# Source tiles of 8 by 16 and column halves for the weighted sums of a local-attention kernel

## The chip, the cores and the metric

The kernel runs on one core of one Trainium2 chip. The engines of that core work side by side: TensorE (PE; PEld is its weight load), VectorE (DVE), ScalarE (ACT), GpSimd (POOL) and SyncE (SP), each of which takes its instructions in the order in which they were written down for it, and DMA queues that are filled by SP and POOL. They meet at semaphores. The metric is the time of one execution on the device in microseconds, as the median of several runs; the profile is one further execution, recorded instruction by instruction.

## The reference

The input x has 4 images of 256 channels and 64 x 64 pixels, all in fp32. Two layers follow.

```python
# layer 0: attention weights from a dilated 7x7 convolution, then a weighted sum of shifted pixels
k = lax.conv_general_dilated(x, w1, window_strides=(1, 1), padding=[(6, 6), (6, 6)],
                             rhs_dilation=(2, 2), dimension_numbers=DN) + b1[None, :, None, None]
k = lax.conv_general_dilated(k, w2, window_strides=(1, 1), padding=[(0, 0), (0, 0)],
                             dimension_numbers=DN) + b2[None, :, None, None]      # 49 logits per pixel
attn = jax.nn.softmax(k, axis=1)
xp = jnp.pad(x, ((0, 0), (0, 0), (6, 6), (6, 6)))
shifts = jnp.stack([xp[:, :, 2*u:2*u + 64, 2*v:2*v + 64] for u in range(7) for v in range(7)], axis=1)
y = jnp.einsum('bkchw,bkhw->bchw', shifts, attn)
# layer 1: whitening in 4 groups of 64 channels (covariance over all pixels, five Newton steps)
```

Each output pixel of layer 0 is the sum of 49 source pixels, two rows or columns apart, weighted by the 49 softmax values of the output pixel. Layer 1 needs the mean and the 64 x 64 covariance of each group over all pixels of y and applies one 64 x 64 matrix per group.

## The kernel before

Because of the dilation of two, rows and columns of one parity only meet their own parity. An image falls into four quarters of 32 x 32 pixels; with 4 images there are 16 quarters, numbered n = 0 to 15. A slot in on-chip memory holds one row parity of one image, `[128, 2, 32, 64]` (channel, channel half, row, column with both column parities); five slots exist, and the results y are written over x in the same slot.

**Logits.** w1 and w2 are folded into one 7x7 kernel with 49 outputs, and the convolution is done by a two-dimensional transform: for each image, a list of row points (`row_eval`), for each of them seven column points (`col_ops`, written to the tiles `xh`), small matmuls on TensorE (`conv_bank`, L538; two groups of 49 output partitions, one per row parity, issued in turn), and the way back on VectorE (`interpolate`, with tiles `pv` and `zz`). One row point, the one at infinity, is done without the column transform by `direct` (L685): 14 terms (7 taps, 2 channel halves) of one matmul of up to 8 x 64 columns for each parity. Image 0 is done first, its row points 0, 4 and 5 also by `direct`; then images 1 to 3 in turn.

**Softmax.** `softmax(b, pc)` brings the logits of one column parity of an image to pixels on partitions (transposes on TensorE, L879), takes the maximum (VectorE), the exponentials (ACT, L893) and multiplies by the reciprocal sum and by `cmask`, which is zero where a column shift would leave the image. The result is a tile `d` with, per pixel, the 49 weights.

**Weighted sums.** For a quarter n, `move_terms` copies the weights of `d` to the tile `zt`, ordered by source row (10 copies, L941 and L953), and one SP DMA writes `zt` to a DRAM buffer `sd[n % 2]`. `load_band` reads it back with a row step one element shorter than it was written (L994, four DMAs for each of three parts), which shifts each source column against the last one, into the tile `band`; a VectorE transpose of 32 x 32 blocks (L1009, one per part) then puts source pixels on partitions and output pixels along the free axis. `make_block(n, m)` transposes 4 source rows of 32 columns of x on TensorE (L1032) and copies them to a tile `xb` (L1040; four buffers), so that source pixels are on partitions there, too. `weighted_sum` (L1061) multiplies the two into PSUM: for each half of 16 output rows five pieces, `PIECES`, each two matmuls, one per channel half. `store_y` (L1080, L1078) evicts the half into the slot, `turn_y` (L1093, L1101) transposes y to pixels on partitions and `moments` (L1114) adds up the covariance.

**The order of the work.** `first_half(n)` and `second_half(n)` write down the order around these parts: which block is made before which sum, and when the next quarter's terms and bands are loaded. They are set between the convolution steps of the next image by a plan with costs; the quarters of images 2 and 3 run partly and wholly after the last convolution, as do `finish` and the tail. TensorE's order is kept as written; on the other engines a scheduler sorts by priority. `load_x` (L130) loads a slot from POOL's queue, image 0 alone by SP's queue at the start. When images 0 and 1 are done, `move` writes slots 0, 1 and 2 out to DRAM (`spill`) and loads the remaining x into them; `bring_back` loads y again at the end. The last stage applies the whitening matrices (L1445, L1461), evicts on ACT and VectorE in turn and stores.

## Time and profile before

| | |
|---|---|
| runs of the kernel (us) | 745.49, 747.77, 745.45; median 745.49 |
| the profiled execution: span (us), taken as its time | 745.9 |
| TensorE busy, share | 704.8 us, 94% |
| VectorE busy, share | 609.9 us, 82% |
| ACT busy, share | 332.0 us, 45% |
| POOL busy, share | 50.8 us, 7% |
| y matmuls (L1061) on TensorE | 154.2 us in 640 records |
| block transposes of the bands (L1009) | 47.5 us, 48 |
| mean granted TensorE clock | 0.980 |

The page of a profile gives the busy time of each engine, then the span in 40 slices, the DMA queues, the chain of work that ended last (followed back from the last instruction, at each step to what released it), and groups of instructions with their mean duration and the idle time ahead of them. Matmuls are pipelined and their ends are modelled, so the busy time of TensorE overlaps; the distance between two starts tells more. Image 0's logits take until about 157 us, the softmax of image 0 and the first weighted sums follow; the last convolution ends at about 580 us, the last weighted sum at 673, the Newton steps at 690.

### The profile page before, as it was taken

The page shows a single profiled execution, that of the slowest core. Times are in us where ns is not written, and L with a number is a line of the kernel's source. Part 1 is how long each engine was busy: PE and PEld are TensorE (multiplying, and loading weights), DVE is VectorE, ACT ScalarE, POOL GpSimd, SP SyncE. Part 2 cuts the span into 40 slices and gives each one's busy share as a digit, 9 for nine tenths or more (in the row PEclk, how much of TensorE's full clock was granted, in tenths as well). Part 3 has the DMA queues.
Part 4 walks back from the last instruction along what each step waited for, and adds up shares of the span by engine and source line. Part 5 has one row for each costly group of instructions (what it writes and reads, how often), then busy time and mean ns, then how long its engine had stood idle before and what let it go on. Part 6 is the DMA issues. An engine that isn't in the chain of part 4 may idle for free.

```text
span 745.9 us, 18571 instructions
## 1 busy us (share of the span) xinstructions
PE 704.8 (94%) x7544; PEld 529.3 (71%) x7544; DVE 609.9 (82%) x1271; ACT 332.0 (45%) x955; POOL 50.8 (7%) x54
## 2 busy tenths in 40 slices
PE   6999999997998897999999999999999889998996
PEld 1449543376898794699998967899998678885331
DVE  3799997999999888877995999799969665545575
ACT  1424340255354443366445344736435563322564
POOL 0410070020000110001000100000000000000000
PEclk9999999999999998999999999999999999997899
DMA  8991110147262392056635920533422143372587
GB/s 322 258 307 73 71 78 19 65 134 227 71 224 91 121 317 62 20 194 211 223 113 172 295 70 2 164 110 111 165 74 86 46 149 107 111 268 103 217 362 323
DMA packets 59629, 114.41 MB, mean 153 GB/s; under 512 B 22887, under 2 KB 42008, under 8 KB 58776
## 3 DMA queue, kind: packets, MB, share of 16 engines
q1 hardware_dynamic: 55848, 94.36, 38.1%
q0 software_dynamic: 3696, 18.88, 7.3%
q8 instruction: 59, 0.97, 0.5%
q14 instruction: 26, 0.21, 0.1%
HBM read 65.88 MB, written 47.33 MB: 152 GB/s over the span
## 4 chain that ended last, share of the span: by engine, by line
PE 66%; DVE 26%; ACT 5%; issue 2%; DMA 1%; SPq 0%; DVEq 0%; ACTq 0%
PE cv L538 22%; PE y L1061 14%; PE acc L685 6%; PE tp L1445 4%; PE tp L1093 3%; PE sig L1114 3%; PE tp L1032 3%; PE cv L685 3%; DVE xh L313 3%; DVE pv L313 2%; DVE zz L313 2%; PE cv L222 2%; DVE ct L313 2%; DVE ct L306 2%; DVE band L1009 2%
## 5 line engine op out<-in xcount | busy, mean ns | idle before, releaser
L538 PE MATMUL cv<-xh,wr 128*49 128x128 f32 x4368 | 249.5, 275 | 5.7 <-DVE rm L899 5.3
L538 PEld LDWEIGHTS cv<-xh,wr 128*49 128x49 f32 x4368 | 243.4, 124 | 9.6 <-ACT xh L494 5.6
L1061 PE MATMUL y<-band,xb 128*128 128x224 f32 (+2 forms) x640 | 154.2, 380 | 8.5 <-ACT xb L1040 6.8
L1061 PEld LDWEIGHTS y<-band,xb 128*128 128x128 f32 x640 | 111.2, 196 | 31.0 <-ACT xb L1040 9.6
L548 ACT COPY pv<-cv 113x486 f32<-113x486 f32 (+1 forms) x63 | 30.0, 476 | 86.5 <-PE cv L538 86.4
L1080 ACT ACTIVATE slot<-y,pivot 128x512 f32<-128x512 f32 x53 | 36.7, 739 | 67.1 <-PE y L1061 67.0
L1101 ACT COPY yt<-tp 128x256 f32<-128x256 f32 x128 | 45.6, 378 | 38.4 <-PE tp L1093 37.0
L313 DVE SCALAR_TENSOR_TENSOR pv<-pv 113x162 f32<-113x162 f32 x186 | 55.4, 322 | 0.8 <-ACT pv L548 0.3
L1032 PE MATMUL tp<-ident,slot 128*128 128x128 f32 x256 | 49.8, 297 | 6.4 <-ACT yt L1101 6.4
L1009 DVE STREAM_TRANSPOSE band<-band 128x864 f32<-128x864 f32 (+1 forms) x48 | 47.5, 992 | 9.7 <-DMA band<-sd 7.3
L1093 PE MATMUL tp<-ident,slot 128*128 128x128 f32 x256 | 51.9, 299 | 3.7 <-ACT yt L1101 1.0
L1093 PEld LDWEIGHTS tp<-ident,slot 128*128 128x128 f32 x256 | 41.2, 205 | 13.8 <-issue 4.2
L1032 PEld LDWEIGHTS tp<-ident,slot 128*128 128x128 f32 x256 | 39.9, 205 | 12.7 <-ACT yt L1101 7.7
L941 ACT COPY zt<-d 32x112 f32<-32x112 f32 (+2 forms) x156 | 44.8, 287 | 1.9
L893 ACT ACTIVATE d<-tp,mx 128x49 f32<-128x49 f32 x128 | 37.0, 336 | 17.4 <-DVE mx L888 13.9
L313 DVE SCALAR_TENSOR_TENSOR xh<-ct 128x512 f32<-128x512 f32 x42 | 27.9, 686 | 13.8 <-PE cv L538 13.4
L1114 PEld LDWEIGHTS sig<-yt 128*64 128x64 f32 x1024 | 32.5, 138 | 6.3 <-issue 4.7
L1114 PE MATMUL sig<-yt 128*64 128x65 f32 x1024 | 36.9, 225 | 0.0
L1040 ACT COPY xb<-tp 128x256 f32<-128x256 f32 x87 | 30.5, 376 | 13.0 <-PE tp L1032 12.5
L1040 DVE COPY xb<-tp 128x256 f32<-128x256 f32 x41 | 16.5, 422 | 22.8 <-PE tp L1032 22.8
L685 PE MATMUL acc<-slot,tap 128*49 128x496 f32 (+3 forms) x168 | 34.6, 569 | 0.0
L893 ACT ACTIVATION_READ_ACCUMULATOR d<-tp,mx 128x1 f32 x128 | 30.7, 241 | 0.0
(228 smaller groups left out, 957.2 us busy)
## 6 DMA issues: line engine op xcount, KB each, us to landing
out_dram<-out SPq DMA_DIRECT2D x32, 512.0 KB, 3.5
sd<-zt SPq DMA_DIRECT2D x16, 896.0 KB, 4.2
slot<-in_x_dram POOLq DMA_DIRECT2D x12, 1024.0 KB, 10.8
band<-sd SPq DMA_DIRECT2D x128, 84.0 KB, 2.1
wr<-gd SPq DMA_DIRECT2D x15, 588.0 KB, 3.7
wr<-gd SPq DMA_DIRECT2D x15, 490.0 KB, 3.9
spill<-slot POOLq DMA_DIRECT2D x3, 2048.0 KB, 7.5
back<-spill SPq DMA_DIRECT2D x3, 2048.0 KB, 13.6
```

Source lines behind the costliest of these rows:

```text
L313: return in_turn(STT(o, a, f, b, ALU.mult, ALU.add))
L538: nc.tensor.matmul(cv[h * HB : h * HB + KT, k, sr : sr + n, sc : sc + n], wv[:, sc, sr, cc], xh[bc][:, :n, h * NCC + cc, :n], start=(j == ...
L685: nc.tensor.matmul(ps[h * HB : h * HB + KT, :, w0:w1_], w[v][:, cc], xs[:, :, cc, w0 + d : w1_ + d], start=(j == 0), stop=(j == len(order) ...
L893: nc.scalar.activation(d[:, h, i], lt[i // NI][:, i % NI, h, :KT], AF.Exp, bias=mx[:, i, h : h + 1], accum_out=s[:, h, i : i + 1],)
L941: ins = nc.scalar.copy(o, i)
L1009: return nc.vector.transpose(f, f)
L1032: nc.tensor.transpose(t[:, cc * P : (cc + 1) * P], xt[:, cc, CR * m : CR * (m + 1), bass.ds(pc, SW, 2)], ident,)
L1040: (nc.vector.tensor_copy if tail else nc.scalar.copy)(xb, t[:, :C])
L1061: nc.tensor.matmul(ps[:, cc, q0 - half * HALF : q1 - half * HALF, :], xb[:, cc * P : (cc + 1) * P], rhs, start=(k == 0), stop=(k == len(PI ...
L1093: nc.tensor.transpose(t[:, cc * P : (cc + 1) * P], yt[:, cc, CR * i : CR * (i + 1), bass.ds(pc, SW, 2)], ident,)
L1101: nc.scalar.copy(yb.rearrange("p a g c -> p (a g) c")[:, :, :GW], t[:, :C].rearrange("p (e c) -> p e c", c=GW),)
L1114: nc.tensor.matmul(sig[g * GW : (g + 1) * GW, cc], yb[:, cc, g, :GW], yb[:, cc, g], start=(count[0] == 0 and cc == 0), stop=(count[0] == 4 ...
```

## The change

The diff touches four things.

- **Tiles of the weighted sums.** Source blocks become 8 rows by 16 columns. A tile (t, h), t = 0 to 3 and h = 0, 1, contributes to 11 output rows and 19 output columns of one half (`ROW0`, `COLS`), so a half has four such pieces; a fifth one, "z", joins the three rows of source that lie over the border between the halves: its block is put together from the lower or upper 64 pixels of the two middle tiles by two further ACT copies.
- **Shift of the terms.** After the softmax, six VectorE shuffles move the weights of the seven column taps by -3 to 3 places within the 32 partitions, in place. `zt` has rows of 22, eight SP DMAs write it to a larger `sd` (cleared once at the start), and `load_band` reads tiles that already have source pixels on partitions: eight DMAs of `[128, 242]` and four of `[64, 3, 19]` per quarter. The block transposes are gone.
- **x in column halves.** A slot is laid out as channel half, column half, row, 32 columns. `load_x` issues four DMAs in place of two; image 0 is first loaded as before and used for its logits, and its two slots are loaded again in the new layout by POOL's queue after `row_eval(0, 5)`. `direct` splits each matmul of images 1 to 3 at the border of the column halves. The last stage reads and writes through views of the halves.
- **Smaller parts.** `row_eval` joins the two channel halves in one instruction for images 1 to 3; `xh` loses its padding column and its clearing on POOL; the eviction of `cv` leaves out the padding of the point at infinity, which makes two ACT copies of one.

```diff
+    TR8, TC = 8, SW // 2
+    WS = 22
+    TROWS = TR8 + R
+    ROW0 = (0, TR8 - R, 2 * TR8, 3 * TR8 - R)
+    COLS = ((0, TC + R), (TC - R, SW))
+    LS = 2 * KS * WS
+    RS = TC * (LS - 1) + WS
+    HS = SH * RS
...
-            queue.dma_start(store[s][:, cc], src[:, :, pr, :])
+            for h in range(2):
+                queue.dma_start(
+                    halves(store[s])[:, cc, h], src[:, :, pr, h * SW : (h + 1) * SW]
+                )
...
-            last = nc.scalar.copy(
-                pv[:K2, slot[b, br], i0 : i0 + len(pts)].rearrange("p n q b -> p (n q b)"),
-                cv[:K2, : len(pts)].rearrange("p n q b two -> p (n q b two)"),
-            )
+            full_ = len(pts) - (INF in pts)
+            nc.scalar.copy(
+                pv[:K2, slot[b, br], i0 : i0 + full_].rearrange("p n q b -> p (n q b)"),
+                cv[:K2, :full_].rearrange("p n q f -> p (n q f)"),
+            )
+            if INF in pts:
+                last = nc.scalar.copy(
...
             for h in range(2):
...
+                    xs = halves(slots[2 * b + h])[:, cc].rearrange("p h (q a) w -> p a h q w", a=4)
+                    parts = []
+                    for g in range(2):
+                        i0, i1 = max(w0 + d, g * SW), min(w1_ + d, (g + 1) * SW)
+                        parts.append(
+                            (i0 - d, i1 - d, xs[:, a, g, :, i0 - g * SW : i1 - g * SW])
+                        )
+                for k, (o0, o1, rhs) in enumerate(parts):
+                    pe(
+                        nc.tensor.matmul(
+                            ps[h * HB : h * HB + KT, :, o0:o1],
+                            w[v][:, cc],
+                            rhs,
...
     row_eval(0, 5, [rb[0], rb[1], xrs[5]])
+    for s in range(2):
+        load_x(s, s, nc.gpsimd)
...
+    for t in sd:
+        flat0 = zt.rearrange("p e w -> p (e w)")
...
+            nc.sync.dma_start(D0[:, f0:f1], flat0[:, : f1 - f0])
...
+        dv = d.rearrange("p h i (u v) -> p (h i u) v", u=KS)
+        for v in range(KS):
+            if v != R:
+                last = nc.vector.stream_shuffle(
+                    dv[:, :, v], dv[:, :, v], [(c - v + R) % SW for c in range(SW)]
+                )
...
-        nc.sync.dma_start(
-            sd[n % 2].rearrange("(p f) -> p f", p=P),
-            zt[:, R : R + NCH * KS].rearrange("p e w -> p (e w)"),
-        )
+        D = sd[n % 2][:]
+        for g in range(CR):
+            for h in range(2):
+                p0 = g * SW + h * TC
+                nc.sync.dma_start(
...
+        for t in (2 * half, 2 * half + 1):
+            e = ROW0[t] - TR8 * t + R
+            for h in range(2):
+                dma = nc.sync.dma_start(
+                    band[:, t, h].rearrange("p r w -> p (r w)"),
+                    bass.AP(
+                        tensor=D.tensor,
+                        offset=D.offset + h * HS + TR8 * t * RS + e * WS + COLS[h][0] - h * TC + R,
+                        ap=[[LS - 1, P], [1, TROWS * WS]],
+                    ),
+                )
...
-        def turn_blocks():
...
-                return nc.vector.transpose(f, f)
...
         xb = bpool.tile([P, C], F32, tag="xb", name=f"xb_{n}_{t8}{h}", bufs=4)
         with tc.high_priority():
             (nc.vector.tensor_copy if tail else nc.scalar.copy)(xb, t[:, :C])
         blocks[n, m] = xb
+        if t8 in (1, 2):
+            z = ("z", 2 - t8)
+            if h == 0:
+                blocks[n, z] = bpool.tile([P, C], F32, tag=f"xbz{t8}", name=f"xbz_{n}_{t8}")
+            i = slice(0, 64) if t8 == 2 else slice(64, P)
+            with tc.high_priority():
+                nc.scalar.copy(blocks[n, z][h * 64 : (h + 1) * 64], t[i, :C])
...
     PIECES = (
-        ((1, 1, 11), (0, 0, 7), (2, 5, 15), (3, 9, 16), (4, 13, 16)),
-        ((4, 16, 23), (3, 16, 19), (5, 17, 27), (6, 21, 31), (7, 25, 32)),
+        ((0, 0), (0, 1), (1, 0), (1, 1), ("z", 0)),
+        (("z", 1), (2, 0), (2, 1), (3, 0), (3, 1)),
     )
...
+        if m[0] == "z":
+            q0, nq = (HALF - R, R) if half == 0 else (0, R)
+            c0, c1 = 0, SW
+            rhs = bandz[:, half].rearrange("p r w -> p (r w)")
+        else:
+            q0, nq = ROW0[m[0]] - HALF * half, TROWS
+            c0, c1 = COLS[m[1]]
+            rhs = band[:, m[0], m[1], :, : c1 - c0]
...
-                    ps[:, cc, q0 - half * HALF : q1 - half * HALF, :],
+                    ps[:, cc, q0 : q0 + nq, c0:c1],
```

## The prediction

> **What bounds the kernel now.** I read the page's busy table first, then the chain of work that ended last, then one busy table over seven stretches, and last the timeline of single stretches, because a modelled "busy" does not tell how fast TensorE issues.
>
> ```profile
> PE 704.8 (94%) x7544; PEld 529.3 (71%) x7544; DVE 609.9 (82%) x1271; ACT 332.0 (45%) x955; POOL 50.8 (7%) x54
> PE 66%; DVE 26%; ACT 5%; issue 2%; DMA 1%; SPq 0%; DVEq 0%; ACTq 0%
> L1009 DVE STREAM_TRANSPOSE band<-band 128x864 f32<-128x864 f32 (+1 forms) x48 | 47.5, 992 | 9.7 <-DMA band<-sd 7.3
> ```
>
> ```profile
> 157.00:188.00 31.00, 25.28 (x430) 24.47 (x427) 31.00 (x62) 17.49 (x86) 5.32 (x7) 0.98 0.65 199
> 188.00:300.00 112.00, 103.39 (x1230) 88.66 (x1228) 105.19 (x232) 51.79 (x132) 7.29 (x9) 0.95 0.43 142
> 300.00:552.00 252.00, 249.13 (x3286) 220.02 (x3283) 219.01 (x433) 126.52 (x409) 7.87 (x6) 1.00 0.44 140
> 552.00:612.00 60.00, 54.54 (x576) 46.56 (x572) 48.41 (x114) 34.39 (x133) 1.14 (x7) 1.00 0.27 82
> 612.00:676.00 64.00, 62.39 (x549) 52.20 (x549) 30.70 (x61) 21.67 (x55) 0.00 (x0) 1.00 0.53 187
> ```
>
> The columns after the length are PE, PEld, DVE, ACT, POOL, granted clock, DMA share, GB/s. From 300 to 552 us and from 612 to 676 us TensorE hardly pauses; from 157 to 188 us VectorE is busy all the time; from 188 to 300 us the two take turns. So a microsecond of TensorE is worth most of a microsecond, a microsecond of VectorE only counts before 300 us. In the timeline, starts tell the issue rate (columns: start, us):
>
> ```profile
> 612.51 1.24 PE L1061 MATMUL y<-band,xb 128*128 128x320 f32 x4
> 613.59 0.39 PE L1093 MATMUL tp<-ident,slot 128*128 128x128 f32 x2
> ...
> 614.06 0.92 PE L1061 MATMUL y<-band,xb 128*128 128x224 f32 x4
> 614.82 0.39 PE L1093 MATMUL tp<-ident,slot 128*128 128x128 f32 x2
> ...
> 616.58 1.37 PE L1061 MATMUL y<-band,xb 128*128 128x224 f32 x8
> 617.88 1.15 PE L1114 MATMUL sig<-yt 128*64 128x65 f32 x32
> ```
>
> Each fp32 matmul leaves two records. Four records of 320 columns take 1.08 us (270 ns each), four of 224 take 0.76 (190 each): 0.845 ns per column either way. The last eight are four of 224 and four of 96: 1.30 - 0.76 = 0.54, so 96 columns cost 135 ns, a floor above 0.845 x 96 = 81. Two more places matter:
>
> ```profile
> 414.38 3.37 POOL L130 DMA_DIRECT2D slot<-in_x_dram  x2 [7.61 <-PE cv L538]
> ```
>
> ```profile
> 429.19 1.05 ACT L448 COPY rb<-slot 128x1024 f32<-128x1024 f32 x1 [1.70 <-DMA slot<-in_x_dram]
> ```
>
> ```profile
> 294.07 11.52 PE cv L685 x56
> ```
>
> ACT, which works in order, already waits 1.70 us for an x load; and one direct convolution of 28 matmuls takes 11.5 us.
>
> **The change part by part.** The profiled execution spans 745.9 us; I take that as its time, 0.4 us above the median of the three runs (745.49). The sum is made against 745.9.
>
> 1. Weighted sums. Before, each of the 32 halves has ten matmuls, two for each piece of 10, 7, 10, 7 and 3 rows of 32 columns: 20 records, 4 x (270 + 190 + 270 + 190 + 135) = 4.22 us. After, eight matmuls of 11 x 19 = 209 columns and two of 3 x 32 = 96: 209 x 0.845 = 177 ns, above the floor; 4 x (4 x 177 + 135) = 3.37 us. Saving 0.85 x 32 = 27.2 us of TensorE. Bounds: the 135 ns floor gives 4 x 5 x 135 = 2.70 us (a gain of 49); the other side is a penalty for runs of 19 columns. The nearest windows in the trace, the 8 x 58 ones of L685, start in pairs 0.387 us apart for 464 columns, 0.83 ns per column, no penalty. I take 27.2.
>
> [...] If a window cost what its 11 full rows of 32 cost (298 ns, an estimate), a half would take 5.31 us and the total would rise by 35 instead of falling by 27.
>
> 2. Direct convolutions of images 1 to 3 (the images are counted from 0) (L685, three times). Each matmul becomes two of one column half, issued first half, second half for one partition group of the output, then both for the other. Before, the two groups alternate and run together: 28 matmuls of 496 columns on average in 11.5 us equal 28 x 2 x 0.845 x 496 / 2. In the new order the second half of a group meets the first of the next, so pairs still run together but wait for the wider part: 2 pairs per term, 2 x 2 x 256 x 0.845 = 0.87 us, 14 terms 12.1, and one unpaired start 0.4: 12.6, so +1.1 x 3 = +3.3 us. No row shows two matmuls of one group in succession beside another group. Bounds: -0.5 us each, and nothing overlapping, 4 x 14 x 248 x 2 x 0.845 = 23.5 us, +36 in all. I take +3.3, as both orders in the trace (L538, L685) overlap completely.
>
> 3. Copies for the middle piece. 64 ACT copies of 64x256, by the row of 128x256 (376 ns) 24 us on ACT, which is 45% busy. TensorE waits only where the last piece of a first half follows its copy: the transpose's result is copied to xb, then to the z block, some 0.2 + 0.27 + 0.38 us, while one pair of 209-column matmuls covers 0.71. About 0.2 us for 12 n (in the last four VectorE copies xb beside ACT), 2.4, and I take 3 for ACT's other work in between; bounds 0 and, if both copies start only when that cover ends, 16 x 0.65 = 10. The cv eviction with the point INF splits in two (569 ns becomes about 430 + 280, x21): the second cv bank hides it.
>
> 4. VectorE. 48 block transposes go (47.5 us). 48 shuffles of 128x112 come, between the 128x56 row of L899 (0.21 us) and the 113x162 row of L313 (0.32): 0.24 each, 12 us. Merging row operations saves 30 pairs x 0.15 = 4. Before 188 us there are 12 shuffles and no transpose: +2.5 us on the path (0 to 3.8). From 188 to 300 us twelve transposes go (11.9 us); TensorE pauses there for some 9 us by the table, not all on VectorE, which limits the gain: -5. After 300 us TensorE covers it. Net -2.5, bounds +4 and -12.
>
> 5. x loads with rows of 128 B, POOL's queue. A 1 MB issue (1.7 us on POOL) becomes two of 4096 pieces each, so four issues per slot: 6.8 us of POOL instead of 3.4. Landing took 10.8 us (page 6). If time goes by bytes nothing is added but 3.4 us of issue, most under the transfer; if by pieces, it doubles, +10.8. The slot-2 load issued at 414.4 ended the ACT wait at 429.2, so all of it lands there; the one issued at 266 is used by ACT at 283.4, some 4 us after it landed. What queues behind that ACT copy: xh, pv evictions, yt copies; TensorE has a bank or so of work, about 4 us. I take +8 us of landing, being nearer to pieces: +4 at image 3, +2 at image 2; bounds 0 and 16. The 4 MB reload of slots 0 and 1 starts after row_eval(0, 5) (about 107 us), with 13.6 us of POOL issues, and is wanted at 194 us: even at 2 x 4 x 10.8 = 86 us it lands in time. The four DMAs that clear sd sit on SP before the weight loads of 162 us: 2.5 MB at the fastest rate in the page's slices (362 GB/s) is 7 us, starting near 157: at most 2 us late where VectorE has the path; nothing.
>
> [...]
>
> 6. SP's queue. Per n 13 issues become 20 (8 for sd, 12 band and bandz loads), 0.43 us each. In the last four n, after a second half: 6 loads 2.6, 8 writes 3.4, landing 2.1 (the 84 KB row), 6 loads 2.6, landing 2.1 = 12.8 us, against 15.7 us per n before and 14.0 after part 1. It fits. With the 4.2 us landing of the old sd write twice it is 17.0, +3 x 4 = 12. At the starts of images, where the softmax waits for shuffles (1.4 us) before zt is moved, I take +1.5.
>
> Sum: -27.2 + 3.3 + 3 - 2.5 + 6 + 1.5 = -16, so 730 us.
>
> **Rivals.** (a) The column halves of the direct convolutions do not overlap: -16 - 3.3 + 36 = +17, 763 us. Place: L685 at 143, 294 and 439 us. For: all three lie in TensorE-bound stretches (11.5 us on the chain at 294). Against: groups overlap fully today. It turns the sign when one costs 5.3 us more than the 1.1 assumed. (b) One of the DMA waits comes at its high end: x loads +10 or SP +12, so 740 to 742. For: the 1.70 us wait at 429 has no slack. Against: POOL is busy 7% of the span, and SP's sum of 12.8 us leaves 1.2 us of slack. (c) Both at once, or a new static order of ACT and SP in which weight loads queue behind band loads: 752. (d) 19-column windows run at the price of full rows: 730 + 62 = 792. Against: the 58-column windows. (e) VectorE's relief counts fully (-12) and POOL's loads go by bytes: 715. (f) The change doesn't bring what it says, for the freed TensorE time turns into waits for VectorE: around 745; against, VectorE is 87% busy from 300 to 552 us and loses 19 transposes (18.8 us) there for 24 shuffles (5.8).
>
> **How the numbers follow.** A measurement of this kernel tells 0.3% (2.2 us) from no change. Forecast 0.52 (own range 719 to 738); (b) 0.11; (e) 0.06; (f) 0.05; (c) 0.12; (a) 0.09; (d) 0.05. Faster: 0.52 + 0.11 + 0.06 = 0.69, less 0.05 because a change that rewrites the order on every engine can hide a cost that no row shows, 0.64; within 0.3%: 0.05; slower 0.31. To leave out no more than 2 in 10 the range goes from 713 to 764, with (a) and (c) inside and (d) outside.
>
> **What would show it.** y records of 128x209 start 177 ns apart; the direct convolutions take 12.6 us each on the chain; half periods in the tail fall from 7.85 to about 7.0 us; the ACT copy rb<-slot of image 3 waits about 9 us for DMA; VectorE is busy some 570 us; shuffles show about 0.24 us. Wrong it would be if direct convolutions show 17 us or more, if y records show over 200 ns, or if TensorE pauses appear ahead of the y matmuls with band or bandz as releaser.

## The result, and the profile after

The changed kernel takes 768.9 us (median; 762.4 to 772.0), the kernel before 745.8 (745.5 to 747.8) beside it: a ratio of 1.028, 95% interval 1.023 to 1.033. It is slower by 23 us, where 730 us and a range of 713 to 764 had been forecast. The profiled execution spans 768.6 us against 745.9. Of the kernels below, e_noshuf, f_shufh and b_shuf also had slow executions (two of four, two of ten and one of four), which the times and ratios given for them leave out.

The page's busy table and, under it, seven columns per stretch as in the prediction (PE, PEld, DVE, ACT, POOL, granted clock, DMA share, GB/s) show a TensorE with less work and more idle time:

```profile
PE 689.3 (90%) x7712; PEld 546.8 (71%) x7712; DVE 593.9 (77%) x1288; ACT 358.1 (47%) x1041; POOL 77.5 (10%) x68
```

```profile
157.00:188.00 31.00, 30.53 (x473) 28.16 (x470) 30.83 (x67) 13.64 (x55) 5.83 (x8) 1.00 0.80 244
188.00:300.00 112.00, 87.19 (x1154) 82.55 (x1151) 94.61 (x216) 55.12 (x169) 8.08 (x10) 0.88 0.48 136
300.00:552.00 252.00, 235.08 (x3162) 216.23 (x3158) 215.97 (x442) 134.09 (x434) 16.30 (x11) 0.97 0.49 133
...
612.00:676.00 64.00, 54.21 (x483) 48.23 (x482) 31.75 (x94) 36.54 (x138) 0.00 (x0) 0.92 0.42 90
```

From 188 to 300 us TensorE was busy 103 of 112 us before and is busy 87 now; from 300 to 552 us it is idle for 17 us where it was for 3, from 612 to 676 us for 10 where it was for 2. The granted clock is lower in the same stretches.

The part that the change is about did what was forecast. In the timeline of the changed kernel (start, duration in us), four records of 209 columns start 0.71 us before the next instruction, 177 ns each:

```profile
671.81 0.87 PE L1148 MATMUL y<-band,xb 128*128 128x209 f32 x4
672.52 0.39 PE L1108 MATMUL tp<-ident,slot 128*128 128x128 f32 x2
```

Where nothing else intervenes (the last three quarters), a quarter takes 13.97 us from first y matmul to first y matmul, against 15.72 before: 1.75 us saved, 28 us over sixteen quarters. I then went from half to half through both traces, and split each stretch into time with a TensorE instruction under way and time without. Over the whole span the time without grew by 38.0 us and the time with fell by 15.3, which makes the 22.6 us of the spans. So if the 27 us were saved, as the last quarters say, then 38 us of new pauses came, and some 12 us of the remaining work ran slower.

The table of what TensorE waited for (us in total, times, longest) names the pauses:

```profile
PE tp L1179 <- ACT yt L1187: 15.4, 8, 3.9
PE cv L574 <- DVE xh L326: 13.9, 2, 7.7
PE cv L574 <- DMA wr<-gd: 10.6, 1, 10.6
PE sig L1200 <- ACT yt L1187: 5.8, 2, 5.1
PE y L1148 <- ACT xb L1114: 5.7, 2, 5.5
PE y L1148 <- ACT xbz L1122: 4.4, 14, 1.4
```

Before, the longest was 5.3 us, and all of TensorE's waits together were 34 us against 71 now. Five places explain most of it.

**Image 0's loads (pause of 6.2 us at 51.6 us).** VectorE, which had its data at once before, waits twice for SP's loads of x, as its timelines show, first of the kernel before, then of the changed one (in brackets the idle time before and what ended it):

```profile
36.73 4.62 DVE L306 TENSOR_TENSOR rb<-slot 128x1024 f32<-128x1024 f32 x4
```

```profile
42.14 2.36 DVE L326 TENSOR_TENSOR rb<-slot 128x1024 f32<-128x1024 f32 x2 [5.33 <-DMA slot<-in_x_dram]
50.54 2.36 DVE L326 TENSOR_TENSOR rb<-slot 128x1024 f32<-128x1024 f32 x2 [6.04 <-DMA slot<-in_x_dram]
```

These loads were not touched. But POOL, which before spent 4.12 us on clearing seven `xh` tiles, now starts its loads of slots 2 and 3 at 29.5 us instead of 33.4, and they move through the same 16 DMA engines (over the span the packets of SP's queue take 41.1% of their time, those of POOL's 11.2%), whose mean busy share from 0 to 60 us is 0.96. POOL's timeline:

```profile
29.52 5.17 POOL L143 DMA_DIRECT2D slot<-in_x_dram  x3
```

**Weights behind bands (10.6 us at 189.8 us).** In the timeline of SP's queue (start, duration) eight `sd` writes and twelve band loads stand ahead of the weights for the next convolution bank. The kernel before comes first, the changed one second:

```profile
169.35 0.32 SPq L954 DMA_DIRECT2D sd<-zt  x1
...
174.34 8.76 SPq L994 DMA_DIRECT2D band<-sd  x12
183.20 11.20 SPq L378 DMA_DIRECT2D wr<-gd  x4
```

```profile
182.50 6.00 SPq L1034 DMA_DIRECT2D sd<-zt  x8
189.48 0.82 SPq L1067 DMA_DIRECT2D band<-sd  x2
...
194.82 1.23 SPq L1078 DMA_DIRECT2D bandz<-sd  x2
196.16 12.30 SPq L398 DMA_DIRECT2D wr<-gd  x4
```

The weights stood behind twelve band loads before, too, and from the first `sd` write to the weights the queue takes as long as it did (13.7 us against 13.9). What is new is that this stretch begins 13 us later: image 0's logits reach TensorE for the softmax 8.3 us later (163.77 us against 155.47), and six shuffles, from 177.07 to 180.52 us, stand between the softmax and `zt`. TensorE itself is only some 8 us late, so it waits 10.6 us; before, it waited 5.3 there, for VectorE.

**Shuffles ahead of ACT's copies (at 349, 495, 624 and 638 us).** At 636 us VectorE starts a softmax's six shuffles, and ACT, which has the `zt` copies of their result next in its fixed order, stands still, with the `yt` copy behind them; that is what TensorE waits for. The timelines of VectorE, ACT and TensorE of the changed kernel in turn:

```profile
635.88 0.57 DVE L971 TENSOR_TENSOR d<-d,rm 128x392 f32<-128x392 f32 x1
636.49 0.01 DVE L977 LOAD_MASK_SELECT d<-d  x1
636.49 0.64 DVE L977 STREAM_SHUFFLE d<-d 128x112 f32<-128x112 f32 x1
...
638.94 0.92 DVE L977 STREAM_SHUFFLE d<-d 128x112 f32<-128x112 f32 x1
```

```profile
639.93 1.78 ACT L1017 COPY zt<-d 32x112 f32<-32x112 f32 x6 [3.67 <-DMA bandz<-sd]
641.62 0.37 ACT L1187 COPY yt<-tp 128x256 f32<-128x256 f32 x1
```

```profile
642.03 0.70 PE L1179 MATMUL tp<-ident,slot 128*128 128x128 f32 x2 [3.89 <-ACT yt L1187]
```

ACT's wait is put down to a DMA, but that had long landed; it ends as the last shuffle does (638.94 + 0.92). The shuffles start 0.55 us apart, not 0.24.

**VectorE behind (5.5 us at 211 us).** Here no `zt` copy is in the way. ACT has a copy to `xh`, which waits for VectorE's `rb`, ahead of the `xb` copy that TensorE needs, and VectorE works without a pause from 196 to 218 us, with six shuffles from 198.85 us on. The timelines of ACT and TensorE:

```profile
208.60 0.65 ACT L1114 COPY xb<-tp 128x256 f32<-128x256 f32 x2
215.92 0.66 ACT L516 COPY xh<-rb 128x512 f32<-128x512 f32 x1 [6.67 <-DVE rb L333]
```

```profile
216.91 1.76 PE L1148 MATMUL y<-band,xb 128*128 128x209 f32 x4 [5.49 <-ACT xb L1114]
```

**A turn-taking of VectorE and TensorE (7.7 us at 254 us).** VectorE's order has changed so that it is idle while TensorE runs the last quarter's sums, and prepares the next bank when TensorE has nothing else. It is there in every version of the changed kernel below, with 2.6 us in e_ztpool and 7.7 to 9.6 us in the others. The half with it is 8.0 us longer than before, the next one 5.5 us shorter, so its net price is some 2.5 us.

A long pause cost more than itself here. After the pauses of 10.6, 5.5 and 7.7 us TensorE's granted clock is 0.50 for 4 to 5 us, as the figure after POOL's busy time shows for the changed kernel around the pause of 211.4 to 216.9 us:

```profile
211.00:217.00 6.00, 0.51 (x5) 0.32 (x3) 5.86 (x6) 1.05 (x3) 0.00 (x0) 0.86 0.02 8
217.00:221.00 4.00, 4.00 (x14) 3.75 (x15) 4.00 (x5) 2.36 (x7) 0.00 (x0) 0.50 0.00 0
221.00:225.00 4.00, 4.00 (x60) 3.67 (x61) 4.00 (x4) 3.61 (x11) 0.00 (x0) 0.86 0.00 0
225.00:229.00 4.00, 4.00 (x70) 3.82 (x64) 4.00 (x7) 3.27 (x11) 0.00 (x0) 1.00 0.41 73
```

From 217 to 221 us 14 matmul records are there, from 225 to 229 us 70. The half with this pause is 7.4 us longer than before, of which 5.5 are the pause and 1.9 slower work.

After a pause of 2.8 us, at 349 us, the granted clock was 0.50 as well:

```profile
352.00:355.00 3.00, 3.00 (x10) 2.61 (x9) 2.35 (x8) 2.26 (x7) 0.00 (x0) 0.50 0.40 69
```

### The profile page after: what moved, and what is told of

Read it like the earlier page. It is cut to its first block, busy times and chain, and to the rows that moved or that the text cites. A ratio compares the mean times of both kernels' runs of the same rounds, so it can differ in the third digit from the quotient of the medians.

```text
span 768.6 us, 19234 instructions
## 1 busy us (share of the span) xinstructions
PE 689.3 (90%) x7712; PEld 546.8 (71%) x7712; DVE 593.9 (77%) x1288; ACT 358.1 (47%) x1041; POOL 77.5 (10%) x68
## 3 DMA queue, kind: packets, MB, share of 16 engines
q1 hardware_dynamic: 84840, 94.42, 41.1%
q0 software_dynamic: 5040, 23.07, 11.2%
## 5 line engine op out<-in xcount | busy, mean ns | idle before, releaser
L574 PE MATMUL cv<-xh,wr 128*49 128x128 f32 x4368 | 249.9, 277 | 25.0 <-DVE xh L326 13.9
L1148 PE MATMUL y<-band,xb 128*128 128x209 f32 x512 | 117.5, 358 | 5.8 <-ACT xb L1114 5.7
L1148 PEld LDWEIGHTS y<-band,xb 128*128 128x128 f32 x512 | 91.6, 203 | 7.3 <-ACT xb L1114 6.4
L1179 PE MATMUL tp<-ident,slot 128*128 128x128 f32 x256 | 53.6, 307 | 19.2 <-ACT yt L1187 15.4
L585 ACT COPY pv<-cv 113x486 f32<-113x486 f32 (+2 forms) x63 | 27.4, 436 | 90.2 <-PE cv L574 80.1
L143 POOL DMA_DIRECT2D slot<-in_x_dram x32 | 54.0, 1692 | 79.9 <-issue 30.8
L1179 PEld LDWEIGHTS tp<-ident,slot 128*128 128x128 f32 x256 | 41.1, 205 | 28.8 <-ACT yt L1187 17.7
L1108 PE MATMUL tp<-ident,slot 128*128 128x128 f32 x256 | 50.8, 304 | 0.0
L958 ACT ACTIVATE d<-tp,mx 128x49 f32<-128x49 f32 x128 | 37.3, 335 | 18.0 <-DVE mx L953 15.5
L1200 PEld LDWEIGHTS sig<-yt 128*64 128x64 f32 x1024 | 33.3, 139 | 12.3 <-ACT yt L1187 6.1
L739 PE MATMUL acc<-slot,tap 128*49 128x256 f32 (+7 forms) x224 | 34.8, 468 | 0.0
L455 ACT ACTIVATE wr<-wr 128x392 f32<-128x392 f32 (+1 forms) x36 | 17.3, 513 | 33.7 <-DVE wr L326 24.0
L326 DVE TENSOR_TENSOR ct<-rb 128x1024 f32<-128x1024 f32 (+1 forms) x24 | 26.6, 1114 | 7.5 <-ACT rb L481 7.1
```

What stands on the lines that cost most here:

```text
L143: queue.dma_start(halves(store[s])[:, cc, h], src[:, :, pr, h * SW : (h + 1) * SW])
L574: nc.tensor.matmul(o, wv[:, sc, sr, cc], xv[bc][:, h * NCC + cc], start=(j == 0), stop=(j == len(terms) - 1), skip_group_check=True,)
L739: nc.tensor.matmul(ps[h * HB : h * HB + KT, :, o0:o1], w[v][:, cc], rhs, start=(j == 0 and k == 0), stop=(j == len(order) - 1), skip_group ...
L958: nc.scalar.activation(d[:, h, i], lt[i // NI][:, i % NI, h, :KT], AF.Exp, bias=mx[:, i, h : h + 1], accum_out=s[:, h, i : i + 1],)
L1108: nc.tensor.transpose(t[:, cc * P : (cc + 1) * P], tile_of(xt, cc, t8, h, pc), ident)
L1148: nc.tensor.matmul(ps[:, cc, q0 : q0 + nq, c0:c1], xb[:, cc * P : (cc + 1) * P], rhs, start=(k == 0), stop=(k == len(PIECES[half]) - 1), s ...
```

## The experiments

All times are medians, beside runs of the kernel before on the same chip (745.8 to 747.7). "The changed kernel" is at 768.9 us; its own runs differ by 10 us and the interval of its ratio spans 7 us, so a gain against it is known to some 5 us.

### e_memset: POOL's loads start later again

```diff
         xh[b] = apool.tile([P, Q8 * 2 * NCC * Q8 * 2], F32, name=f"xh{b}")
+        nc.gpsimd.memset(xh[b], 0.0)
```

> The changed kernel with the seven xh memsets put back on POOL ahead of its x loads of slots 2 and 3; the order on every other engine stays as it is. Theory A (the loads of slots 2 and 3 start some 4 us earlier once these memsets are gone, and share the DMA engines with SP's loads of image 0): the loads start near 33 us instead of 29.5, SP's loads of image 0 end near 38 to 40 us instead of 49.96, the two DVE waits of 5.33 and 6.04 us for slot<-in_x_dram nearly go, the first y matmul comes 6 to 8 us earlier, and the total falls by as much, to about 762 us. Rival (image 0's loads are late for another reason, or the time is lost again behind them): loads end near 50 us still, total within 2 us of 768.9.

Measured: 758.4 us, ratio to before 1.017 (1.012 to 1.022): 10.5 us less by the medians, by this one edit, which adds work to POOL and changes no other engine's order. In its profile POOL's loads start at 32.7 us, and VectorE's first wait is gone; the second remains:

```profile
36.74 2.36 DVE L327 TENSOR_TENSOR rb<-slot 128x1024 f32<-128x1024 f32 x2
45.59 2.36 DVE L327 TENSOR_TENSOR rb<-slot 128x1024 f32<-128x1024 f32 x2 [6.49 <-DMA slot<-in_x_dram]
```

Theory A holds in the main, though image 0's last load still lands near 45 us, not 38 to 40. TensorE's pause falls from 6.2 to 1.2 us and the first y matmul comes 4.9 us earlier; the two profiled spans differ by 6.0 us, so 6 of the 10.5 us are seen in a trace. In the other kernels that keep the early loads, the same pause took 2.9, 5.8, 7.1 and 10.3 us (e_ztpool, e_vmajor, e_noshuf, e_wrpool); in others with this edit VectorE's second wait took 0, 0.5, 3.1 and 4.2 us (e_three, f_vmajor, f_pool, f_shufh). Whether it depends on how the two streams of packets meet, and makes up a part of the changed kernel's spread of 10 us between runs, was not shown.

### b_half: column halves of x in the kernel before

```diff
-            queue.dma_start(store[s][:, cc], src[:, :, pr, :])
+            for h in range(2):
+                c = slice(h * SW, (h + 1) * SW)
+                queue.dma_start(store[s][:, cc, :, c], src[:, :, pr, c])
```

> The kernel before with one thing of the change: each x load of POOL is issued as two column halves, so in pieces of 128 B instead of 256 B, into the old layout; no other engine's order changes. Theory by pieces: the POOL packets of 4096 B take 278 ns as in the changed kernel instead of 194, a slot lands some 5 to 10 us later, the ACT copy rb<-slot of image 3 waits 6 to 10 us instead of 1.70, and the total rises by 4 to 8 us to 750 to 754. Theory by bytes, or hidden: the wait grows by no more than 3.4 us (the issue time of two more DMAs) and the total stays within 2 us of 745.8.

Measured: 749.9 us, ratio 1.0038 (1.0019 to 1.0056), so 2.9 us more. The ACT copy of image 3 waits 3.82 us instead of 1.70:

```profile
431.38 1.05 ACT L450 COPY rb<-slot 128x1024 f32<-128x1024 f32 x1 [3.82 <-DMA slot<-in_x_dram]
```

It lies between the two theories. The wait grew by 2.1 us, within the 3.4 us of issue time; the total moved by more than "hidden" allows. Pieces of half the size did not cost twice the time: POOL's packets of 4096 B took 274 ns on average in the changed kernel, which loads the same pieces, and 203 before, a third more. In the changed kernel the same copy waits 4.79 us.

### e_noshuf: no shuffles

```diff
-        for v in range(KS):
+        for v in range(0):
             if v != R:
                 last = nc.vector.stream_shuffle(
```

> The changed kernel without the 48 partition shuffles (so the terms of each column are not shifted, and the weighted sums use wrong weights); the rest is computed as before. Theory B (each softmax's six shuffles take 3.1 us on VectorE, not 1.4, the zt copies in ACT's fixed order wait for them, and behind those the yt copies that TensorE needs): the TensorE pauses for yt at 349, 495, 624 and 638 us (2.8, 3.3, 1.8, 3.9 us) go, the total falls by 8 to 14 us, to 755 to 761. Rival (the shuffles are covered by TensorE's work, as the prediction had it; the pauses move to another releaser): the total falls by at most 3 us.

Measured: 737.2 us (733.4 and 741.1), ratio 0.987 (0.979 to 0.995); over all four runs the median is 743.3, the figure that later expectations start from. Leaving the shuffles out gives 31.7 us by the one and 25.6 by the other, at least twice what Theory B expected; VectorE's busy time falls by 25.1. By place, in the profiled execution (747.9 us), from half to half against the changed kernel: 7.6 us at the second half of the sums (the pause at 211 us), 7.0 at 493 to 545 us, 9.0 at 612 to 649. The edit also changes the order on VectorE, ACT and SP, so a part of this can be the order. The pause at 349 us is the one that merely moved: 2.8 us stand at 353 us, with the next convolution bank as the waiting step.

### e_wrpool: image 1's weights on POOL's queue

```diff
-            nc.sync.dma_start(wt, gd[br][:, s0 : s0 + ns])
+            (nc.gpsimd if b == 1 else nc.sync).dma_start(wt, gd[br][:, s0 : s0 + ns])
```

> The changed kernel with the weight loads of image 1 (wr<-gd) issued by POOL instead of SP. Theory C (the weights wait in SP's queue behind eight sd writes and the band loads of image 0): the 10.6 us pause of TensorE at 189.8 us falls to about 5, the wait that the kernel before has there on VectorE; total falls by 4 to 6 us, to about 764. Rival (the transfer itself is late, or VectorE would have held TensorE as long): the pause stays at 9 to 11 us under another releaser, total within 2 us of 768.9.

Measured: 757.6 us, ratio 1.012 (1.006 to 1.019): 11.3 us less, above the 4 to 6 of Theory C. The pause at 189.8 us is halved, as expected, which is 5.7 us, and the one of 5.5 us at 211 us is gone as well. The edit also changes the fixed orders of VectorE and ACT, so what the second part is due to stays open. The line of TensorE's timeline with the first pause:

```profile
198.95 7.64 PE L574 MATMUL cv<-xh,wr 128*49 128x128 f32 x96 [4.96 <-issue]
```

### e_ztpool and f_pool: the zt copies on POOL

```diff
-                    ins = nc.scalar.copy(o, i)
-                    if after is not None:
+                    ins = nc.gpsimd.tensor_copy(o, i)
+                    if False:
```

The second line takes away an order that some of these copies had been given on ACT. f_pool has this together with the edits of e_memset and e_wrpool.

> The changed kernel with all of ACT's zt copies (terms to the staging tile) made by POOL; the shuffles stay on VectorE. It tells apart how the 25.6 us come that leaving the shuffles out gave. Theory B1 (ACT's fixed order: yt and xb copies stand behind zt copies that wait for the shuffles): TensorE's pauses for yt at 349, 495, 624 and 638 us (2.8, 3.3, 1.8, 3.9 us) go, total falls by 8 to 14 us to 755 to 761. Rival B2 (the shuffles' own 3.1 us of VectorE per softmax, 25 us for eight, count directly): the pauses stay with VectorE as releaser, total within 3 us of 768.9.

> The changed kernel with the xh memsets back, image 1's weight loads on POOL's queue, and the zt copies on POOL; everything is computed. Theory A + C + B1: 768.9 - 10.5 - 11.3 - 10 = 737, faster than the kernel before (747). Rival (POOL's copies are slower than ACT's, or stand behind its weight and x loads, so that bands come late): y matmuls wait for band<-sd, total 748 or more.

Measured: 774.3 us for e_ztpool, ratio 1.039 (1.033 to 1.045), and 765.8 for f_pool, 1.027 (1.023 to 1.030). The remedy failed for a reason that the rival of f_pool had named in part: POOL's copies took 723 ns on average against ACT's 289, so `zt` was ready later. But it was not the y matmuls that waited for their bands; the weights stood behind them in SP's queue. In e_ztpool the chain reads from POOL to SP:

```profile
177.35 17.59 POOL L1017 COPY zt<-d 128x56 f32<-128x56 f32 x11 [14.32 <-DVE d L977]
```

```profile
190.86 6.98 SPq L1034 DMA_DIRECT2D sd<-zt  x8
...
208.35 1.49 SPq L398 DMA_DIRECT2D wr<-gd  x3
```

TensorE paused 27.0 us there, for `wr`. The pauses for `yt` at 349, 495, 624 and 638 us did go, but 9.0 and 4.2 us at 356 and 508 us came in their place, ahead of convolutions that wait for weights, and 2.9 us at 639 us for `xbz`. So it does not decide between B1 and B2; it confirms C once more, with the other sign.

### e_three: the three causes taken away together

The edits of e_memset, e_wrpool and e_noshuf in one kernel.

> Three edits in one: the xh memsets back on POOL, image 1's weight loads on POOL's queue, and the shuffles left out (so the weighted sums use unshifted terms). If the three causes are separate, their gains add: 10.5 + 11.3 + 25.6 = 47.4, total 721 to 723. If they overlap (the 5.5 us pause at 211 us went both without shuffles and with the weights on POOL, 7.6 us of y offset each), total 728 to 732. Rival (TensorE's granted clock, 0.951 against 0.980, is a cost of its own): total not under 738, clock still at 0.95.

Measured: 725.5 us, ratio 0.973 (0.970 to 0.976), and a clock of 0.974. Singly the edits gave 47.4 to 53.5 us, by the two figures for e_noshuf, together 43.4: largely separate causes with an overlap of 4 to 10 us (the pause at 211 us, 7.6 us, counts in two of them). The rival falls: the clock came back with the pauses' end. Without the three, the change is worth 21 us, more than the forecast of 16, and this with shuffles left out.

### f_shufh, f_defer, f_noz: when the shuffles are made, and the copies for the middle piece

f_shufh (with the edits of e_memset and e_wrpool) makes the shuffles per half of a softmax:

```diff
-        dv = d.rearrange("p h i (u v) -> p (h i u) v", u=KS)
+            dv = d[:, h].rearrange("p i (u v) -> p (i u) v", u=KS)
```

f_defer also moves those of the second half into `second_half`:

```diff
+        if n % 4 < 2:
+            shuffle(n // 4, n % 4, 1)
         turn_y(n, 0)
```

f_noz is f_defer with the z copies taken out:

```diff
-        xb = blocks[n, m]
+        xb = blocks[n, {("z", 0): (1, 1), ("z", 1): (2, 0)}.get(m, m)]
...
-        if t8 in (1, 2):
+        if t8 in ():
```

> The changed kernel with the xh memsets back, image 1's weight loads on POOL's queue, and each softmax's shuffles made in two groups of six of 128x56, the first right after its half is normalized; everything is computed. If what counts is how soon the first half's terms can be copied to zt: 768.9 - 21.8 = 747 less up to 6 us, 741 to 747. Rival (a shuffle's price is mostly fixed, so twelve of them take 4.5 to 6 us per softmax instead of 3.1): 750 to 760.

> The changed kernel with the xh memsets back, image 1's weight loads on POOL's queue, and the shuffles in groups of six of 128x56 for half a softmax: those of the first half right after it is normalized, those of the second half only in the second half of the n two before they are wanted, when TensorE has other work. Everything is computed. If the shuffles cost by what waits for them at an image's start (some 20 of the 25.6 us, as the first half alone still costs f_shufh 744.2 against 725.5 without shuffles), putting half of them under cover gives half of these 18.7 us back: 733 to 738. Rival (their place does not matter, VectorE's own 0.3 us each times 96 does): 742 to 746, as f_shufh.

> As f_defer, but without the copies that gather the two middle pieces (the z pieces multiply the block of a neighbouring tile instead, so four rows and more of each half get wrong sums): the price of the 64 copies. By TensorE's waits for xbz (4.4 us for y, 2.3 for tp in the changed kernel) 5 to 8 us below f_defer; by the prediction's term, 3 us below; if the waits only move to the next releaser, within 1.5 us of it.

Measured: f_shufh 743.8 us, ratio 0.9964 (0.9940 to 0.9988); f_defer 742.4, 0.9942 (0.9922 to 0.9962); f_noz 736.5, 0.9854 (0.9825 to 0.9884). With two queues put right the changed kernel, all computed, is a little below the kernel before. Putting half of the shuffles elsewhere gave 1.4 us, which the two intervals do not tell from nothing, and not the 6 to 11 expected; VectorE's busy time is 595.5 and 595.3 us, the same. But the edit moved them far in image 0 only (to 207 and 225 us, from 171 and 194); in images 1 to 3 the second group begins 1.4 to 7.6 us after the first has ended, against 1.4 to 6.2 in f_shufh. So whether their place matters stays open. The copies for the middle piece cost 5.8 us, about what the waits for `xbz` show, where the prediction had 3.

### b_shuf2, b_shufout, b_copy, b_strout: what six instructions per softmax cost the kernel before

b_shuf and b_shuf2 are the same kernel; each partition is mapped to itself, so only time is added, in the chain from softmax to bands:

```diff
+        dv = d.rearrange("p h i (u v) -> p (h i u) v", u=KS)
+        for v in range(KS):
+            if v != R:
+                last = nc.vector.stream_shuffle(dv[:, :, v], dv[:, :, v], list(range(SW)))
```

b_copy has `tensor_copy` in place of the shuffle; b_shufout shuffles a contiguous tile of zeros, and b_strout one with steps of seven elements, both read by nobody else.

> The kernel before with six shuffles per softmax added after the normalization, in place and with each partition mapped to itself (the result is unchanged); the 48 block transposes stay. Theory B (in the chain softmax, zt, sd, band, y the shuffles' 3.1 us per softmax is paid at the images' starts): the total rises by 10 to 25 us over 746. Rival (it is the new static order that makes them cost, not the place): at most 4 us.

> The kernel before with six in-place shuffles per softmax that map each partition to itself, once more, for a look at where the 36 us are. By the first time: 780 to 786 us. Theory P (place: the chain softmax, zt, sd, band, y): TensorE's added pauses stand at the first y of each image and at the copies behind zt. Theory V (VectorE's time): the added pauses are ahead of cv matmuls whose inputs VectorE makes, before 300 us above all.

> The kernel before with six in-place copies of the same 128x112 shapes in the place of the shuffles (some 0.2 us each, 1.2 us per softmax, against 3.1). If the price goes by the time that they add, in the chain or on VectorE: about a third of 36 us, 755 to 762. If more instructions there mean a worse fixed order whatever they take: 772 to 784. If only the shuffle itself is dear: within 3 us of 747.

> The kernel before with the same number of shuffles of 128x112 per softmax on a tile of zeros that nothing else reads, so that no later step waits for them but VectorE's own order. Theory P: at most 5 us over 747. Theory V: the same 25 to 36 us as in the chain, 772 to 783.

> The kernel before with six shuffles per softmax on a tile of zeros that nothing else reads, now on 112 elements seven apart (28 B, over 112 neighbouring elements), so that they take as long as those of the change, off the chain of the bands. If time on VectorE is what they cost: 0.4 to 0.55 us each, 20 to 26 us of VectorE, total +20 to +37 (766 to 783). If the chain is what makes them cost: at most 10 us over 746. If the stride does not set their price: VectorE's busy time rises by 8 us as in b_shufout, total 752 to 755.

| kernel | time (us) | ratio to before | more than before (us) | VectorE's busy time added (us) |
|---|---|---|---|---|
| b_shuf | 783.6 | 1.047 (1.045 to 1.049) | 35.9 | |
| b_shuf2, shuffles in the chain | 783.1 | 1.049 (1.045 to 1.052) | 37.3 | 25.7 |
| b_copy, copies in the chain | 760.5 | 1.020 (1.017 to 1.023) | 14.6 | 8.4 |
| b_strout, strided shuffles off the chain | 763.7 | 1.024 (1.022 to 1.027) | 17.4 | 22.1 |
| b_shufout, contiguous ones off the chain | 753.6 | 1.010 (1.009 to 1.012) | 7.8 | 7.8 |

Both theories hold a half. Off the chain a microsecond of VectorE cost 0.8 to 1.0 us, in it 1.45 to 1.7. The two are not at the same place, though: in the chain the 48 instructions run from 168 to 641 us, six after each softmax, but those that nobody reads were all put between 162 and 346 us (b_strout). And the order on VectorE and ACT differs between the two kinds. Only b_strout and b_shufout have the same order on every engine: there 14.3 us more of VectorE cost 10.1 us. What the chain by itself adds is therefore not shown by these runs alone. In b_shuf2 the waits are those of the chain, with ACT's `yt` copies and the weights in front:

```profile
PE tp L1036 <- ACT yt L1105: 20.3, 10, 5.2
PE cv L538 <- DMA wr<-gd: 8.2, 1, 8.2
PE y L1065 <- DVE band L1013: 5.3, 1, 5.3
```

That the kernel before takes 37 us of harm from shuffles alone also shows that they need nothing else of the change to be dear; b_copy, which puts as many instructions at the same places, bounds what a new order alone can cost at 14.6 us. And the groups of the four kernels (busy us, mean ns of one), b_shuf2, b_shufout, b_strout and b_copy in turn, show that the layout sets their price:

```profile
L912 DVE STREAM_SHUFFLE d<-d 128x112 f32<-128x112 f32 x48 | 27.3, 878 | 0.0
```

```profile
L914 DVE STREAM_SHUFFLE scratch<-scratch 128x112 f32<-128x112 f32 x48 | 13.3, 276 | 0.0
```

```profile
L915 DVE STREAM_SHUFFLE scratch<-scratch 128x112 f32<-128x112 f32 x48 | 31.1, 648 | 0.0
```

```profile
L912 DVE COPY d<-d 128x112 f32<-128x112 f32 x48 | 9.1, 262 | 0.1
```

The same 112 elements take 276 ns in a row and 648 ns seven apart; a copy of the strided view takes 262 ns, so it is the shuffle that the stride makes slow.

### b_notr: what the block transposes were worth

```diff
-        if n == 0:
-            held.append(turn_blocks)
-        else:
-            turn_blocks()
```

> The kernel before without its 48 block transposes (the bands stay unturned, so the weighted sums use wrong weights; the rest is computed). The prediction valued them at 47.5 us of VectorE, of which some 5 before 300 us and up to 12 would count. Balance of the terms measured so far: about 6 us below 747, 739 to 743. Rival (in the chain they are as dear as the shuffles): 725 or less. Rival (all covered): within 2 us.

Measured: 739.0 us, ratio 0.992 (0.988 to 0.995), 6.8 us less, though VectorE's busy time falls by 41 us. It is the figure that the balance of the other terms had asked for. Here a microsecond of VectorE was worth 0.17 us: most of the transposes' time lies beside other work, as the prediction had it.

### e_vmajor and f_vmajor: the shuffles on contiguous rows

The terms are stored with the column offset v outermost; the copies to `zt` read them with the larger step.

```diff
-        d = terms[b, pc] = bpool.tile([P, 2, NCH, KT], F32, tag="d", name=f"d_{nm}", bufs=2)
+        d = terms[b, pc] = bpool.tile([P, KS, 2, NCH, KS], F32, tag="d", name=f"d_{nm}", bufs=2)
...
-                    d[:, h, i], lt[i // NI][:, i % NI, h, :KT], AF.Exp,
+                    d[:, :, h, i].rearrange("p v u -> p u v"),
+                    lt[i // NI][:, i % NI, h, :KT].rearrange("p (u v) -> p u v", u=KS), AF.Exp,
...
-                    dv[:, :, v], dv[:, :, v], [(c - v + R) % SW for c in range(SW)]
+                dv = d[:, v].rearrange("p h i u -> p (h i u)")
+                last = nc.vector.stream_shuffle(dv, dv, [(c - v + R) % SW for c in range(SW)])
```

f_vmajor adds the edits of e_memset and e_wrpool.

> The changed kernel with the softmax's terms stored with the column offset outermost, so that each shuffle works on 112 elements in a row instead of 112 elements seven apart; all else as in the change, everything is computed. On a contiguous tile (b_shufout) a shuffle of 128x112 took 0.276 us, in the seven-apart layout 0.65 to 0.95, 0.55 from start to start. Theory (the shuffles cost by the time that they add in the chain, and the stride doubles it): VectorE's busy time falls by 10 to 18 us from 593.9, the total by 10 to 18 us to 751 to 759. Rival (a shuffle has its price whatever the layout, for instance from loading its mask): VectorE's busy time within 4 us, total within 4 us of 768.9.

> The same layout together with the xh memsets back on POOL and image 1's weight loads on POOL's queue; everything is computed. Without any shuffle these two gave 725.5. Six shuffles of 0.16 to 0.28 us add 1.0 to 1.7 us per softmax to the chain, by the measure of b_copy (14.6 us for 9.1 us of VectorE) 12 to 20 us: no more than 738, and at best 730. If the causes add as they did so far (10.5 + 11.3 + the gain of e_vmajor): 733 to 737.

Measured: e_vmajor 754.2 us, ratio 1.013 (1.008 to 1.017), 14.8 us below the changed kernel; VectorE's busy time is 578.3 us, 15.6 less. The rival falls. This is the cleanest of the runs on the shuffles: the order of instructions is that of the changed kernel on every engine, and the main difference is how long the shuffles take. A microsecond of them in the chain cost 0.95 us here. The shuffles now start 0.19 us apart, with their masks loaded as before:

```profile
336.22 0.28 DVE L984 STREAM_SHUFFLE d<-d 128x112 f32<-128x112 f32 x1
336.41 0.02 DVE L984 LOAD_MASK_SELECT d<-d  x1
336.41 0.28 DVE L984 STREAM_SHUFFLE d<-d 128x112 f32<-128x112 f32 x1
```

f_vmajor takes 735.9 us, ratio 0.9861 (0.9837 to 0.9884), with everything computed: 33 us below the changed kernel and 10 below the kernel before. It is the version to keep. The causes add again: 10.5 + 11.3 + 14.8 = 36.6 singly, 33.1 together. The shuffles that are left cost 10.4 us against e_three. What TensorE still waits for in it:

```profile
PE cv L575 <- DVE xh L327: 11.2, 2, 7.7
PE tp L1185 <- ACT yt L1193: 6.1, 5, 2.4
```

Of the first, 7.7 us are the turn-taking of VectorE and TensorE. Whether another order of VectorE would remove it was not tried.

## Why the prediction was wrong

| step of the prediction | forecast (us) | measured (us) | from |
|---|---|---|---|
| 1 weighted sums | -27.2 | about -27 | 1.75 us per quarter in the undisturbed last ones |
| 2 direct convolutions | +3.3 | about +0.4 at full clock | 11.66 us for the first of the three, against 11.52 before |
| 3 copies for the middle piece | +3 | +5.8 | f_defer less f_noz |
| 4 VectorE: transposes that go | counted within -2.5 | -6.8 | b_notr |
| 4 VectorE: shuffles that come | 12 us of work, within -2.5 | +25.6 to +31.7 | e_noshuf |
| 5 x loads in smaller pieces | +6 | +2.9 | b_half |
| 5 start of POOL's loads | not priced | +10.5 (6.0 in the traces) | e_memset |
| 6 SP's queue | +1.5 | +11.3, of which 5.7 are the wait for the weights | e_wrpool |
| sum | -16 | +23 to +29 | the two kernels: +23.2 |

Less the overlap of 4 to 10 us in e_three, some 19 us are left to set against 23.2. With medians that are known to some 5 us, that the sum is this good is partly luck; that nothing large is missing is not.

**What held.** Step 1, with 177 ns per record; windows of 19 columns in rows of 32 ran at the rate of contiguous ones (0.847 ns per column against 0.845). No slowing by these windows is seen. Rival (d) is out. Step 2's bound of +36 us and rival (a) are out as well, since the column halves overlap completely. The timeline of the changed kernel (start, duration in us) has one direct convolution, 11.66 us against 11.52 before:

```profile
152.18 11.66 PE L739 MATMUL acc<-slot,tap 128*49 128x256 f32 x112
```

The one of image 3 took 11.70 us; the one of image 2, right after the pause at 306 us, took 13.22, with the granted clock at 0.52 from 311 to 318 us. None of the three signs of being wrong that the prediction named came up: the direct convolutions, the y records, and TensorE's waits, none of which is for a band. The pauses came where it had not looked. In step 5, "+4 at image 3" was too high: the ACT wait grew from 1.70 to 4.79 us, where about 9 had been expected, and TensorE's pause behind it is 1.7 us. At image 2, where 2 had been put, the same ACT copy waits 7.6 us and TensorE 5.1 behind it; with later loads in the beginning (e_memset) TensorE waits 2.2 there. How the one comes from the other was not followed up.

**The step that failed first: the shuffles in step 4.** "0.24 each, 12 us", between the rows of a contiguous 128x56 operation and of a 113x162 one. Neither row was a shuffle nor had a stride of seven elements; the strided shuffle starts every 0.55 us, 27.4 us of busy time in all. The bound was wrong too: the other VectorE instructions of the trace say little about what a shuffle takes on a strided view. And "after 300 us TensorE covers it" was wrong in kind. TensorE covered VectorE's time only where nothing that it needed stood behind VectorE's result on a third engine. ACT's fixed order has `zt` copies, which wait for the shuffles, ahead of `yt` copies, which TensorE needs; the four pauses of that kind in the trace are 11.7 us long. The prediction asked of moved steps what is queued behind them, and did so for SP and for ACT's x copy, but not for ACT's `zt` copies.

**The step left out: a removed instruction that had held something back.** The seven memsets were costed at nothing, as POOL is 7% busy. They kept POOL's loads of slots 2 and 3 away from image 0's loads, by 4 us, on a stretch where the DMA engines are busy nearly all the time (0.96) and VectorE waits for the data. The prediction looked for what a removed instruction costs, not for what it delays.

**Step 6, the SP queue.** In the tail the sum per quarter (12.8 us) fits: a quarter takes 13.97 us, with no wait for a band. But the queue was summed where no weights stand in it. At image 0's first bands a weight load that TensorE waits for stands behind eight writes and twelve loads, and these begin 13 us later than before, because the loads of image 0 and the shuffles hold `zt` back; 1.5 us had been put for that. Rival (c) comes closest, "a new static order of ACT and SP in which weight loads queue behind band loads", priced at 752 us with a chance of 0.12. The wait is the one that it names, but the order was there before, and the lateness was new; the shuffles' true cost and the clock it did not have.

**The clock.** The prediction took pauses at their length. TensorE's half clock after them added some 12 us to 38. The clock records say the same: half of the time that TensorE was busy at 0.50 is 12.3 us before and 26.0 in the changed kernel, 13.7 more.

**The range.** Its upper end, 764, was rival (a)'s; rival (c) joined the x loads and the queue, but none of the cases held the shuffles, the memsets and the queue at once.

## What to carry to other kernels

Of a removed instruction ask not only what it cost but what it kept waiting: work on an idle engine can be the only thing that keeps two streams of transfers apart (here seven memsets, 4.12 us in all; putting them back gave 10.5 us). When an operation is put into a chain that an in-order engine reads from, look at what stands behind the reader; that, and not only the busy share of the engine that does the new work, sets its price (here 0.95 to 1.7 us per microsecond in the chain and 0.7 to 1.0 off it, measured at different places of the kernel; the block transposes that went were worth 0.17). And before a whole change is given up, take its parts back one at a time: three edits, none of which touches the idea, turned 768.9 us into 735.9.

## What the runs showed of the hardware

- A shuffle within 32 partitions took 276 to 280 ns for 128x112 elements in a row (0.19 us from start to start) and 648 ns or more for elements seven apart (0.55 us from start to start), while a copy of the same strided view took 262 ns.
- After pauses of 5.5 and 7.7 us the granted clock was 0.50 for 4 us and more (217 to 221 us, and the same from 262 to 266 us), and after one of 2.8 us for 3 us and more (352 to 355 us).
- POOL's copies of the terms took 723 ns on average in e_ztpool where ACT's took 289 in the changed kernel.
- ACT's copies to `zt` took 376 ns on average in f_vmajor, reading with the large step, against 289 in the changed kernel: 13.5 us more of ACT, which the gain on VectorE outweighed.
- Two matmuls in succession into one group of output partitions, beside two into the other, cost nothing against the alternation of the groups: 11.66 us for 56 matmuls of half the columns, 11.52 for 28 of the whole.
